# Attention convolutions from six products per four output columns, with the input planes stored by their producer

## The chip, the core and the metric

The kernel runs on one core of one Trainium2 chip, in one launch. The metric is the device time of that core in microseconds (us); lower is better. The core has a matrix engine (TensorE, called PE in the profile), a vector engine (VectorE, DVE), a scalar engine (ScalarE, ACT), a general engine (GpSimd, POOL) and a queue engine that here only issues transfers (SyncE, SP). Each works through its own list of instructions in order. TensorE reads its operands from the on-chip memory (SBUF) and writes into accumulator banks (PSUM); the other results go through SBUF. DRAM tensors are reached by DMA only.

## What is computed

Two layers are applied to four images of 96 channels by 128 x 128 pixels, all in float32. The first is a state-space block (projection, a 3x3 depthwise convolution, four scans over the image, a layer norm, an output projection). The second, where the change lies, is this, for every image on its own:

```python
def _attn_conv(x1, x2, aw1, aw2, aw3):          # C = 96, K = 3, pad = 1
    key = unfold_nonoverlap(conv2d(x1, aw1))    # 3x3 patches, 42 x 42 of them
    qry = unfold_nonoverlap(conv2d(x2, aw2))
    attn = einsum("bckl,bqkl->bqck", key, qry)  # one 96 x 96 matrix per tap
    attn = softmax(attn.reshape(B, C, C * 9) / sqrt(C * 9), axis=2)
    value = conv2d(x1, aw3)
    return conv2d(value, attn.reshape(B, C, C, 3, 3))   # weights of this image
xr, x1, x2 = relu_split_norm(x)
y1 = layer_norm(_attn_conv(x1, x2, aw1, aw2, aw3))
y2 = layer_norm(conv2d(x2, w_conv2)) * x1
out = xr + conv2d(concat([y1, y2]), w_full) + b_full    # 1x1
```

So an image needs five 3x3 convolutions of 96 to 96 channels: aw1 and aw3 on x1, aw2 and w_conv2 on x2, and the last one on `value`, with weights that are known only when the first four are done.

## The kernel before

**Two halves of the program.** In the first half the projections of the four images run beside the scans, then the output norm of image 0 (`ssm_output`, `split_norm`) and its four convolutions (`direct_maps`, nine plain taps) beside the rest of the scans. In this half `in_order` fixes each engine's list to the order of emission. In the second half each image b gets an `attention(b)` on the "left", and beside it a "light" stream: `attn_output(b-1)` (through `close`) and then `ssm_output(b+1)` and `split_norm(b+1)` (through `norm`). `co_run(left, right, pace)` interleaves the two: every generator yields the cost of what it has emitted, and the right one gets pace times the cost of the left one; whatever is left of the light stream is emitted alone afterwards. Here the framework's scheduler may move instructions, with the emission order as priority. Image 0 needs only the last convolution in its `attention`, as `direct_maps` has done the others (`img.mapped`).

**Convolutions before.** `attention` makes two output columns from four products in place of six taps' worth of multiplications. The 96 input channels times three rows (288 contraction rows) are stacked as 128 + 128 + 32 partitions. `load_rows` brings six rows of a padded map (`x1d`, `x2d`, `vd`: rows of PW = 129) into three tiles `y0`, `y1`, `y2`, already shifted by rows; `columns` makes the four column combinations in the tiles `t0`, `t1`, `t2`, on GpSimd (L1269 to L1271) and VectorE (L1276, L1278; for the value map L1269 too). `products` runs, for each of four products, two full matmuls (L1293, PSUM tile `bank`), and then the four 32-row rests in four row groups of the array (L1304). `outputs` copies one bank to SBUF on ScalarE (L1342) and combines four banks with four VectorE instructions (L1334 to L1337). A "pair set" of 12 rows of one map takes two passes with 128 output channels (one chunk of six rows each), and one with the other 64 channels of both chunks side by side in the array's columns. Weights carry `wd` in their name for the pairs and `wa` for the last convolution. The float32 matmul shows as two instructions in the trace.

**Attention matrix.** `Taps` keeps the key and query rows in `ring` tiles, turns nine rows of patches at a time (`turned`: 18 transposes per group, L1388, copied by ScalarE as `kt`, L1393) and multiplies them (`multiplied`, L1403, added to `sm` by L1414). `weights` takes the softmax and makes the product weights; the last pass of the w_conv2 channels is held back (`taps.rest`) and emitted between the softmax and the transposes of the weights.

**PSUM.** In the second half the left pool has six tiles of one bank (`bank`), and the light stream's pool two.

**split_norm.** It has two loops over 16 pieces of eight rows: one for the sums (L1082 to L1089), one that writes the positive half `x1` and the negative half `x2` (ScalarE L1165, VectorE L1170, store on ScalarE's DMA queue).

Of the kernel before, what the change touches and what calls it, by code (L numbers as in the profile page):

```python
# [17 lines left out]
C = 96  # L18
H = W = 128
L = H * W  # L20
CH = 512
# [8 lines left out]
PW = W + 1  # L30
AR = 12
CR = AR // 2
GROUP = 9
NG = H // GROUP
RING = 4 * GROUP // 3
NSTRIP = (H + AR - 1) // AR

# [25 lines left out]
def kernel(  # L63
# [853 lines left out]
    def ssm_output(b, yms, xnew, stats, ps, side):  # L917
# [5 lines left out]
        with tc.tile_pool(name="c2", bufs=2, side=side) as p2:  # L923
# [10 lines left out]
            def squares(c):  # L934
                sq = p2.tile([C, 2, SN], F32, name="sq", bufs=1)
                for j in range(2):
                    nc.scalar.activation(sq[:, j], ys[c][:, j], AF.Square)
                sums_of[c] = sq, bank(ps)

            def sums(c, j):  # L940
                sq, pm = sums_of[c]
                for g in range(4):
                    nc.tensor.matmul(
                        pm[32 * g : 32 * g + 32],
                        lhsT=mean192[:, 0:32],
                        rhs=(ys[c], sq)[g % 2][:, j, bass.ts(g // 2, CH)],
                        start=(j == 0),
                        stop=(j == 1),
                    )

# [50 lines left out]
            for c in range(NS + 2):  # L1001
# [5 lines left out]
                if new:  # L1007
                    squares(c)
# [30 lines left out]
    def split_norm(xnew, x1d, x2d, stats, keep, cnt, ps, side):  # L1039


        with tc.tile_pool(name="n2", bufs=2, side=side) as p2:
            ahead = []

            def piece(t):
                if t < NS:
                    y = p2.tile([C, SN], F32, name="xn", bufs=4)
# [29 lines left out]
            later = Later()  # L1077
            for i in range(NS):
# [9 lines left out]
                z = p2.tile([C, SN], F32, name="xz")  # L1088
# [3 lines left out]
            later.flush()  # L1092
            for i in range(3):
# [62 lines left out]

            for i in range(NS):
# [3 lines left out]
                for side_, m in ((0, x1d), (1, x2d)):  # L1161
                    h = p2.tile([C, RS, PW], F32, name=f"half{side_}")
                    nc.gpsimd.memset(h[:, :, 0:1], 0.0)
                    to = h[:, :, 1:PW]
# [8 lines left out]
                    at = (i * RS + 1) * PW  # L1173
                    later(lambda m=m, at=at, h=h: nc.scalar.dma_start(
                        m[:, at : at + RS * PW], h.rearrange("p h w -> p (h w)")
                    ), 1)
                later.tick()
                yield 3.5
# [8 lines left out]


# [3 lines left out]
    def products_weights(wt, v, s):  # L1192

        nc.vector.tensor_copy(wt[:, :, 0:2], v[:, :, 0:3:2])
        nc.vector.tensor_add(s, v[:, :, 0], v[:, :, 2])
        nc.vector.tensor_scalar(s, s, 0.5, None, ALU.mult)
        for i, sign in ((2, 0.5), (3, -0.5)):
            nc.vector.scalar_tensor_tensor(wt[:, :, i], v[:, :, 1], sign, s, ALU.mult, ALU.add)

    def pair_weights():  # L1200
# [4 lines left out]
        with tc.tile_pool(name="wq", bufs=2, side="right") as pw:  # L1205
            for pair in ((aw1, aw3), (aw2, w_conv2)):
                g = pw.tile([C, 3, 3, 2, C], F32, name="g")
                for j, src in enumerate(pair):
                    v = src.rearrange("c (h w) o -> c h w o", w=3)
                    for w in range(3):  # L1210

                        nc.sync.dma_start(g[:, :, w, j], v[:, :, w if j else 2 - w])
                taps.append(g)
            yield
            for i, g in enumerate(taps):
                g = g.rearrange("p h w j o -> p h w (j o)")
                wt = pw.tile([C, 3, 4, 2 * C], F32, name="wt")
# [25 lines left out]
    def load_rows(pool, m, r0, r):  # L1243


        n = r * PW + 1
        tiles = [pool.tile([128, CR * PW + 4], F32, name=f"y{i}", tag=f"y{i}") for i in range(3)]
        for y, parts in zip(tiles, STACK[:2]):
            for p, c0, c1, dh, _ in parts:
                at = (r0 + dh) * PW  # L1250
                nc.sync.dma_start(y[p : p + c1 - c0, :n], m[c0:c1, at : at + n])
        at = (r0 + 2) * PW
        nc.sync.dma_start(tiles[2][0:32, :n], m[64:96, at : at + n])
        for p in range(32, 128, 32):
            nc.sync.dma_start(tiles[2][p : p + 32, : n - 1], m[64:96, at + 1 : at + n])
        return tiles

    def columns(pool, tiles, r, first):

        def of(t, k, p0=0, p1=128):  # L1260
# [717 lines left out]
```

## Time and profile before

| | |
|---|---|
| device time, three runs | 6721.16 us median (6720.42 to 6732.53) |
| profiled execution, first to last instruction | 6729.0 us; its time outside the span is not shown |
| PE busy | 5618.7 us (84%), 22236 matmuls |
| DVE busy | 4792.1 us (71%) |
| ACT busy | 2985.5 us (44%) |
| POOL busy | 3802.7 us (57%) |
| DMA | 1226.28 MB, mean 182 GB/s |
| mean granted PE clock | 0.900 |

Busy time is the time in which the engine executes at least one instruction; for PE the ends are modelled, so it is an upper view. The granted clock is the share of full speed that the matrix engine was allowed. The second half starts at about 3606 us; the image-specific convolution (weights `wa`) of images 0, 1, 2 and 3 runs at 3608 to 3812, 4654 to 4804, 5660 to 5820 and 6461 to 6609 us, and ahead of each of the last three lies the pairs stage of that image (from 3815, 4820 and 5840 us).

### The profile page before, as it was taken

To read this page: it belongs to the slowest core of one execution; us is meant where nothing else is said; L and a number is where in the kernel's file an instruction comes from. 1 tells how busy PE (TensorE), PEld (TensorE's weight loads), DVE (VectorE), ACT (ScalarE), POOL (GpSimd) and SP (SyncE) were. 2 spreads that over 40 slices of the span, in tenths; PEclk is the share of its full clock that TensorE was granted. 3 is DMA by queue.
4 is the path that set the end of the run, shared out by engine and by line. 5 is a ranking of instruction groups with operands and counts; after the bars stand their busy time and mean duration, and the time that the engine had idled before them with its cause. 6 is when DMAs were issued, how large, how long until landed. Compare 5 with 4: busy or idle time off the path is not lost. (4 is left out here: it accounts for less than half of the span.)

```text
span 6729.0 us, 74614 instructions
## 1 busy us (share of the span) xinstructions
PE 5618.7 (84%) x22236; PEld 2323.3 (35%) x22236; DVE 4792.1 (71%) x6588; ACT 2985.5 (44%) x3749; POOL 3802.7 (57%) x2568
## 2 busy tenths in 40 slices
PE   5989978878886618989996988987988987988987
PEld 2323323322221104444342433433333443334442
DVE  3257879979896578889537776658776658775578
ACT  1357767777875566677434112233122233121112
POOL 2236758879796438889423634545644445545561
PEclk9999989989996659999997989998989998999998
DMA  6766777866765666765668666657666657664566
GB/s 166 174 155 187 199 212 198 227 168 179 220 179 165 187 191 191 207 187 169 198 186 235 182 172 161 185 146 232 165 179 166 176 153 233 168 182 125 135 169 183
DMA packets 796126, 1226.28 MB, mean 182 GB/s; under 512 B 218702, under 2 KB 558678, under 8 KB 783244
## 3 DMA queue, kind: packets, MB, share of 16 engines
q1 hardware_dynamic: 761740, 1129.63, 61.7%
q10 hardware_dynamic: 17776, 53.47, 2.5%
q0 software_dynamic: 16208, 38.42, 2.1%
q8 instruction: 179, 2.93, 0.2%
q14 instruction: 223, 1.83, 0.1%
HBM read 856.79 MB, written 295.13 MB: 171 GB/s over the span
## 5 line engine op out<-in xcount | busy, mean ns | idle before, releaser
L615 PE MATMUL bank<-y,wp 128*128 128x512 f32 (+3 forms) x3584 | 1317.5, 625 | 72.4 <-DMA y<-y 34.2
L1293 PE MATMUL bank<-t,wd 128*128 128x384 f32 (+2 forms) x4224 | 1175.4, 507 | 61.6 <-ACT s L1342 23.0
L848 POOL TENSOR_TENSOR y<-y,dl 128x1024 f32<-128x1024 f32 x384 | 1054.5, 2746 | 244.9 <-DVE dl L840 220.4
L815 POOL TENSOR_TENSOR dl<-dl,u 128x1024 f32<-128x1024 f32 x384 | 1008.2, 2625 | 253.6 <-ACT dA L791 119.0
L1269 POOL TENSOR_TENSOR t<-y 128x768 f32<-128x768 f32 (+1 forms) x352 | 572.0, 1625 | 780.8 <-DMA y<-x1d 280.5
L836 DVE TENSOR_TENSOR_SCAN dA<-dA,pBC 128x512 f32<-128x512 f32 x768 | 981.7, 1278 | 31.5 <-DVE pBC L819 0.5
L1342 ACT COPY s<-bank 128x384 f32<-128x384 f32 (+2 forms) x292 | 135.5, 464 | 1718.8 <-PE bank L1304 1606.6
L1293 PEld LDWEIGHTS bank<-t,wd 128*128 128x128 f32 (+1 forms) x4224 | 579.9, 175 | 609.0 <-issue 352.5
L729 PE MATMUL pBC<-xr,wbc 60*128 60x512 bf16 (+1 forms) x1536 | 459.8, 402 | 354.3 <-DVE dA L836 281.0
L840 DVE TENSOR_TENSOR dl<-dA,pBC 128x512 f32<-128x512 f32 x768 | 528.8, 689 | 269.6 <-PE pBC L729 196.8
L615 PEld LDWEIGHTS bank<-y,wp 128*128 128x128 f32 (+3 forms) x3584 | 458.7, 169 | 742.2 <-issue 652.8
L1661 PE MATMUL bank<-y,wn 128*128 128x384 f32 (+5 forms) x2408 | 673.4, 507 | 40.5 <-ACT ring L1675 15.9
L1293 PE MATMUL bank<-t,wa 128*96 128x384 f32 (+1 forms) x1408 | 497.6, 500 | 97.0 <-POOL t L1270 36.0
L658 ACT ACTIVATE dl<-pd,dtb 128x512 f32<-128x512 f32 x768 | 485.6, 684 | 184.6 <-PE pd L729 169.4
L1270 POOL TENSOR_TENSOR t<-y 128x384 f32<-128x384 f32 (+1 forms) x440 | 457.1, 1039 | 147.3 <-DMA y<-vd 68.3
L819 DVE TENSOR_TENSOR pBC<-dl,pBC 128x512 f32<-128x512 f32 x768 | 527.1, 686 | 7.7 <-POOL dl L815 6.0
L1334 DVE TENSOR_TENSOR d<-s,bank 128x384 f32<-128x384 f32 (+2 forms) x292 | 156.1, 535 | 520.1 <-ACT s L1342 492.1
L1271 POOL TENSOR_TENSOR t<-y 128x384 f32<-128x384 f32 (+1 forms) x440 | 442.7, 1006 | 0.0
L1661 PEld LDWEIGHTS bank<-y,wn 128*128 128x128 f32 (+3 forms) x2408 | 308.1, 168 | 340.5 <-issue 172.4
L791 ACT ACTIVATE dA<-dl,negA 128x1024 f32<-128x1024 f32 x384 | 420.3, 1141 | 2.3
L729 PEld LDWEIGHTS <-wbc 60*128 60x128 bf16 (+1 forms) x1536 | 104.0, 96 | 789.3 <-issue 775.3
L658 ACT ACT_TABLE_LOAD x245 | 314.3, 1283 | 100.9 <-PE pd L729 93.9
(255 smaller groups left out, 7774.4 us busy)
## 6 DMA issues: line engine op xcount, KB each, us to landing
u<-zb SPq DMA_DIRECT2D x192, 1024.0 KB
yms<-y SPq DMA_DIRECT2D x96, 512.0 KB
y<-yms SPq DMA_DIRECT2D x64, 768.0 KB
xn<-xnew SPq DMA_DIRECT2D x128, 384.0 KB
y<-y SPq DMA_DIRECT2D x128, 258.2 KB
zb<-z SPq DMA_DIRECT2D x64, 512.0 KB
y<-vd SPq DMA_DIRECT2D x168, 193.8 KB
y<-in_x SPq DMA_DIRECT2D x56, 480.0 KB
```

The source lines that it names most:

```text
L615: nc.tensor.matmul(blocks(pz[p:e]), lhsT=ws[k][:, d, c : c + e - p], rhs=window(ys[k], at, d, n), start=(i == 0), stop=(i == len(terms) - 1),)
L658: nc.scalar.activation(dst, src, AF.Softplus, bias=bias)
L729: nc.tensor.matmul(p, lhsT=w[rows], rhs=xr[rows, at : at + CH], start=True, stop=True)
L815: nc.gpsimd.tensor_mul(t, t, u_view(n))
L819: nc.vector.tensor_mul(p, live[n]["dl"][:, bass.ts(half, CH)], p)
L836: nc.vector.tensor_tensor_scan(h, h, p, init, ALU.mult, ALU.add)
L840: nc.vector.tensor_mul(live[n]["dl"][:, sl], live[n]["dA"][:, sl], live[n]["C", half])
L848: nc.gpsimd.tensor_add(v, v, t.rearrange("p (a b) -> p a b", b=W))
L1269: eng.tensor_sub(v[:, 0:2], of(y, 0), of(y, 2))
L1270: nc.gpsimd.tensor_add(v[:, 2], of(y, 0)[:, 1], of(y, 2)[:, 0])
L1293: nc.tensor.matmul(pc[p:e, :n], lhsT=w[:, i, c : c + e - p], rhs=t[k][:, i, :n], start=(k == 0), stop=False,)
L1661: nc.tensor.matmul(pc[p:e, :n].rearrange("p (h w) -> p h w", w=W), lhsT=w[:, c : c + e - p], rhs=v[:, :, 0:W], start=(i == 0), stop=(i == ...
```

## The change

**Arithmetic.** Four output columns are made from six products (points 0, 1, -1, 2, -2 and infinity) where two were made from four. Every 3x3 weight becomes 3 x 6 (`NP = 6`) in place of 3 x 4.

**Producer makes the planes.** The six column combinations of an input map ("planes", 33 column groups each per row, with padding) are computed once by `planes_of`, four ScalarE scalings and seven GpSimd additions or subtractions per piece, and stored in DRAM tensors `x1p`, `x2p`, `vp` of [96, 6, 131, 33]. For images 1 to 3 `split_norm` does it for x1 and x2 (two maps, 16 pieces of eight rows), and `attention` does it for `value` (pieces of six rows). Image 0 keeps its maps as before; in its `attention` a new function `lift` reads `vd` in pieces of four rows and makes the planes.

**Consumer.** A chunk is 12 rows. Its loads are four: one of 96 channels x 6 planes x 14 rows into `ya`, one of 32 channels, and two small ones into `yc`; the second 128-row stack `yb` is made from `ya` by two ScalarE copies of 64 x 2376 elements. The load of chunk c + 2 is emitted after the last product of chunk c. `columns` and its instructions are gone.

**Products, PSUM and evacuation.** `products` runs four of the six, their rests, then two and their rests; PSUM on the left is three tiles of two banks. `outputs` takes one ScalarE copy of two banks, two VectorE instructions over two banks, then a few over one (see the diff). One temporary tile `sd`, one output tile `oc`.

**Attention matrix.** Patches are turned six rows at a time (21 groups where there were 14), the two maps' transposes share one PSUM tile and one ScalarE copy; the products of two groups accumulate in PSUM. Nothing is held back for the softmax any more.

**Around it.** `squares` makes one half at a time in a single half-size tile (its second half after the first sums); `xn` has three buffers for four and `xz` one for two; channel order in the 32 + 64 split is swapped; 18 stores of zeros are added near the start; the pace of the light stream is 0.85 where it was 0.6.

```diff
+TW = 4; NP = TW + 2; TN = W // TW; PT = TN + 1; PP = PT * TW; AA = 2.0
...
-            def squares(c):
-                sq = p2.tile([C, 2, SN], F32, name="sq", bufs=1)
-                for j in range(2):
-                    nc.scalar.activation(sq[:, j], ys[c][:, j], AF.Square)
+            def squares(c, j):
+                sq = p2.tile([C, SN], F32, name="sq", bufs=1)
+                nc.scalar.activation(sq, ys[c][:, j], AF.Square)
...
             def sums(c, j):
...
+                if j == 0:
+                    squares(c, 1)
...
+            def stored(i, m, h):                       # split_norm
+                if planes:
+                    return planes_of(
+                        later, p2, h, RS, lambda pl: store_planes(nc.scalar, m, i * RS, RS, pl)
+                    )
...
-                later.tick()
-                yield 3.5
+                for _ in range(6 if planes else 1):
+                    later.tick()
+                    yield 2.0 if planes else 3.5
...
+    def planes_of(later, pool, t, r, then, most=RS):
...
+            nc.scalar.mul(eo, by_k(1), a2)
+            nc.gpsimd.tensor_sub(df, by_k(2, TW), by_k(0, TW))
...
+            nc.scalar.mul(pl[:, 0:NP:5], df[:, 0:2], a2)
+            nc.scalar.mul(pl[:, 3], df[:, 1], AA)
+            nc.gpsimd.tensor_sub(eo, by_k(3), eo)
+            nc.gpsimd.tensor_add(pl[:, 1], eo[:, 1], eo[:, 0])
+            nc.gpsimd.tensor_sub(pl[:, 2], eo[:, 1], eo[:, 0])
...
+            nc.gpsimd.tensor_sub(pl[:, 0:NP:5], df[:, 2:4], pl[:, 0:NP:5])
+            nc.gpsimd.tensor_sub(pl[:, 4], df[:, 2], pl[:, 3])
+            nc.gpsimd.tensor_add(pl[:, 3], df[:, 2], pl[:, 3])
+            then(pl)
...
+        a, b = pairs_of(ps), pairs_of(ps)              # products
+        to = {1: a[:, 0], 3: a[:, 1], 2: b[:, 0], 4: b[:, 1]}
+        for i, _ in FOUR:
+            main(to[i], i)
+            later.tick()
+            yield 1.3 * share
+        rest(0, FOUR, to)
+        sums, finish = evac
+        sums(a, b)
...
+        c = pairs_of(ps)
+        to = {0: c[:, 0], 5: c[:, 1]}
+        for i, _ in TWO:
+            main(to[i], i)
...
+        rest(1, TWO, to)
+        finish(c)
...
+                nc.scalar.copy(got[0][:, 0], a[:m, :, :n])      # outputs
...
+                nc.vector.tensor_sub(d, s, b[:m, :, :n])
+                nc.vector.tensor_add(s, s, b[:m, :, :n])
+                for p, e, v in parts:
+                    for k, x, f in ((1, d, AA), (2, s, AA * AA)):
+                        nc.vector.scalar_tensor_tensor(
+                            at(v, k), rows(x[p:e, 1]), f, rows(x[p:e, 0]), ALU.mult, ALU.add
+                        )
+                nc.vector.tensor_add(s[:, 0], s[:, 0], s[:, 1])
+                nc.vector.scalar_tensor_tensor(
+                    d[:, 0], d[:, 1], AA * AA * AA, d[:, 0], ALU.mult, ALU.add
+                )
...
+                    nc.vector.tensor_add(
+                        to,
+                        got[0][p:e, :, 0].rearrange(of, t=TN),
+                        c[p:e, :, :n].rearrange(of, t=TN),
+                    )
...
+                    for p, e, c0, h, k in ((0, 96, 0, 0, 2), (96, 128, 64, 1, 1)):   # load
+                        to = ya[p:e, :, : (r + k) * PT]
+                        src = maps[m][c0 : c0 + e - p, :, r0 + h : r0 + h + r + k]
+                        nc.sync.dma_start(to, src.rearrange("c i h t -> c i (h t)"))
...
+                    yb = p2.tile([128, NP, AR * PT], F32, name="yb")                 # turn
+                    for h in (1, 2):
+                        nc.scalar.copy(
+                            yb[64 * h - 64 : 64 * h, :, :n], ya[0:64, :, h * PT : h * PT + n]
+                        )
...
+            def lift(i):
...
+                for a in range(r0, r0 + r, 4):
+                    h = p2.tile([C, 4 * PP + 4], F32, name="lift")
...
+                    own(planes_of(
+                        own, p2, h, 4, lambda pl, a=a: store_planes(nc.sync, img.vp, a, 4, pl), 4
+                    ))
...
-    psl = ctx.enter_context(tc.tile_pool(name="psa", bufs=6, space=PSUM, side="left"))
+    psl = ctx.enter_context(tc.tile_pool(name="psa", bufs=3, space=PSUM, side="left"))
...
-        co_run(left, light, 0.6 if b else 1.5)
+        co_run(left, light, 0.85 if b else 1.5)
```

## Prediction

> **What bounds the kernel now.** I read the page first, then the windows of image 1's two stages, then the groups and waits inside them, then the timeline. Windows (stretch, length, busy time and count of PE, PEld, DVE, ACT, POOL; granted clock; DMA share; GB/s) of its pairs stage and its last convolution:
>
> ```profile
> 3820.00:4640.00 820.00, 695.60 (x3124) 324.56 (x3122) 538.70 (x783) 236.70 (x333) 350.57 (x351) 0.91 0.64 173
> 4654.00:4804.00 150.00, 145.81 (x526) 62.72 (x528) 134.65 (x196) 15.89 (x27) 111.52 (x97) 0.99 0.71 200
> ```
>
> TensorE is busy 85% and 97% of the two, ScalarE 29% and 11%. The groups of the whole page that the change cuts (busy us, mean ns; idle before them and its releasers):
>
> ```profile
> L1293 PE MATMUL bank<-t,wd 128*128 128x384 f32 (+2 forms) x4224 | 1175.4, 507 | 61.6 <-ACT s L1342 23.0 <-DVE s L1335 19.1 <-DVE sm L1414 16.2
> ...
> L1293 PE MATMUL bank<-t,wa 128*96 128x384 f32 (+1 forms) x1408 | 497.6, 500 | 97.0 <-POOL t L1270 36.0 <-DMA wa<-ring 24.4 <-DVE t L1276 11.9
> ```
>
> Waits of the pairs stage (who for whom: us, times, longest):
>
> ```profile
> POOL t L1269 <- DMA y<-x1d: 111.2, 7, 26.6
> ...
> PE bank L1403 <- ACT kt L1393: 24.1, 13, 7.7
> ...
> PE bank L1765 <- DVE c L1754: 21.0, 10, 4.0
> ```
>
> and those of the SP queue:
>
> ```profile
> SPq L1486 <- DVE ring L1337: 170.7, 16, 18.2
> ```
>
> TensorE waits in many small pieces, on PSUM copies and on VectorE. GpSimd waits for loads, 26.6 us at the longest, behind an SP queue that stores hold for up to 18.2 us; TensorE hardly feels it, since columns are made ahead. Last, the timeline of the last convolution:
>
> ```profile
> 4779.97 2.82 PE L1293 MATMUL bank<-t,wa 128*96 128x384 f32 x8
> 4782.72 0.89 PE L1304 MATMUL bank<-t,wa 32*96 32x384 f32 x4
> 4783.53 2.82 PE L1293 MATMUL bank<-t,wa 128*96 128x384 f32 x8
> ```
>
> From start to start, eight instructions take 2.75 us and two rests 0.81, without a gap: 12 rows take 4 x 3.56 = 14.2 us.
>
> **What the Trainium skill says.** "TensorE: Matmul & The Clock Gate", Part 3 (packing small matmuls): matmuls in different row or column groups of the array run together. The trace agrees: 32 instructions of 64 columns took 5.38 us where 16 of 128 took 5.33. "SBUF — State Buffer", "SBUF: two separate sides": a VectorE instruction with two SBUF inputs and a GpSimd one lock each other out for their whole length. It agrees: L1276 takes 0.48 to 0.57 us where I looked at single ones, and 1.05 in the mean of the pairs stage. "GPSIMD Engine Reference", 3.1: about 2.6 cycles an element with two inputs, 2.2 ns at the page's 1.2 GHz. Here it is less: in the pairs stage L1270 (384 elements) takes 0.974 us and L1269 (768) 1.566, so 1.54 ns an element and 0.38 us per instruction, which I use.
>
> **TensorE.** Six products per four columns stream 0.75 of the columns of four per two: 0.25 x (1175.4 + 497.6) = -418 us, that is 98 in each of three pairs stages and 31 in each of four last convolutions. The rests (L1304) go from one group per two columns to two per four: nothing. Patches of six rows make 378 transposes and 189 multiplications an image for 252 and 126; L1388 and L1403 are busy 43.0 and 33.2 us in image 1's stage, so half more is 38. The marginal time is less (five transposes 0.82 us, four 0.62), some 26. I take 35: 63 remain per pairs stage, -189 in all.
>
> **VectorE.** Gone: L1276 and L1278, 94 us in the pairs stage and 40 in the last convolution, with 23 of L1269 there. Added, per 12 rows of 128 outputs: three instructions of 768 elements, estimated 0.95 us each (0.537 for 384 and 0.679 for 512 in L1334 and L994), and four of 384 out of SBUF at 0.6 to 1.0; 5.3 to 6.9 against 4.3. The pass of 64 takes 2.8 to 5 against 2.1. Per set of 12 rows of one map 10.7 us of old work becomes 8 to 12. So VectorE gets no relief beside `attn_output`, whose L1753 to L1760 (101 us) and L1766 (23) fill it: TensorE's gain is partly lost there, +10 a stage (0 to 20): +30.
>
> **GpSimd.** Gone: 302 us of columns in the pairs stage (L1269 to L1271), 114 in the last convolution. Added: eight rows of planes are 3168 elements in seven instructions, 7.5 us, x 32 = 241 an image; value planes 22 x 6.3 = 139. The sum falls, but it moves: the second `split_norm` loop emits 192 units for 56, so the light stream (463, against 526 x 0.85 = 447) now lasts through the last convolution, and 16 units remain to run alone: about 10 us twice, +20 (0 to 40). Image 0: `lift` is 32 x 5.1 = 163 us of GpSimd, and some 60 of image 1's planes come late, against a stage of 204 us: -30 to +40, I take 0.
>
> **ScalarE.** Added per image: `yb`, 66 copies of 2376 elements; 0.464 us for 384 and 1.048 for 1024 give 0.91 ns an element, 2.3 us each, 152 us. Plane scalings 77, `kt` 10, the value's 32-channel copy 16: 255 on 253. TensorE keeps its old cover only while the PSUM copy comes in time, and now `yb` waits for a load on the engine that also empties PSUM, with the light stream's instructions behind it and TensorE waiting for a tile. Between a rest and the next need of its tile lie 2 to 6 us of matmuls. Price: 0 to 145 us an image (all of GpSimd's waits on x1d and x2d loads, 111.2 and 33.5). I take 20, as loads are asked for some 25 us ahead in the pairs: +60. The three PSUM tiles of two banks belong to this term.
>
> **Loads and the last convolution.** Loads carry 1.5 MB per 12 rows in four issues, where 2.4 MB went in 16; SP gets lighter. But with two `ya` the load of chunk c + 2 waits for the end of chunk c. Landing takes about 3 us (192 KB 3.7, 384 KB 4.3) and 1.5 MB takes 5.0 to 8.6 us (at 299 GB/s, the busiest slice of the pairs stage, to 173); then come 4.6 of `yb`. TensorE needs 3 x 2.75 + 2 x 0.81 = 9.9 us a chunk. Two chunks per (12.6 to 16.2) + 9.9: 11.3 to 13 each, 124 to 143 us for 148. That is -15 for image 3. For 1 and 2 the light stream's planes (some 17 pieces, 128 us of GpSimd) and the single `oc` tile make it 13 to 15 a chunk: 0 (-20 to +15 each).
>
> **Rest.** The pass kept back for the softmax (7.3 us) no longer covers it: 3 x 8 = +24. Halved `squares` put a wait of ScalarE on TensorE into image 0's norm, where the order is fixed: 0 to 3 us x 16 pieces, I take 1: +16. Zero stores are 10368 packets of 132 bytes on SP; at the mean 87 ns (61.7% of 16 x 6729 us over 761740) 0 to 56 us, I take 15. Fewer `xn` and `xz` buffers, swapped channels, product weights: 0, hidden by the slow steps of `split_norm`; without that cover 10.
>
> **Sum.** -189 + 30 + 20 + 60 - 15 + 24 + 16 + 15 = -39. The profiled span, 6729.0, is 7.8 us (0.1%) over the median of the runs; no time outside it is shown. Put on the median: 6721 - 39, about 6680 us.
>
> **Rivals.** All of TensorE's gain arrives: -189 - 124 + 55 (softmax, squares, zeros), 6460 us. For it: no other engine's sum exceeds TensorE's. Against: the load chain above. Slower, by ScalarE's order: the PSUM copy into `sd` stands behind the next chunk's `yb`, which stands behind its load, and half of GpSimd's 145 us reaches TensorE, 72 x 3 = 216 in place of 60: 6680 + 156, about 6840. It decides from 0.9 us of stall a chunk on (99 us over 110 chunks). For it: the wait of 26.6 us; against it: the lead of 25. GpSimd bounds the second `split_norm` loop: 15 us for a piece of both maps against about 14 of other work, 48 pieces, +48: 6730. That the change doesn't do what it says I exclude: the counts are in the code.
>
> **Numbers.** A measurement of this kernel can tell about 0.2% (13 us) from no change. Chances: the likeliest 0.35 (own range 6560 to 6705), the full gain 0.14, GpSimd's or another even balance 0.07, ScalarE's order or several prices at their upper ends 0.44. The range, 6470 to 6890, reaches from nearly the full gain over the slower case.
>
> **What would show it.** Right: the main matmuls of pairs and last convolutions busy near 1255 us together; transposes 1386 for 1008; ScalarE over half busy in the pairs stages; last convolutions at 11 to 15 us a chunk. Wrong: TensorE waiting for the copy into `sd` for more than 60 us a stage (slower), last convolutions at 9.9 us a chunk (faster), or image 0's stages longer by more than 40.

## Result and the profile after

The change makes the kernel slower: 6996.59 us (6989.58 to 7007.83, four runs) against 6725.15 (6720.42 to 6732.53, four runs), a ratio of 1.0402 with a 95% interval of 1.0386 to 1.0417. The forecast was 6680, and the range ended at 6890. The profiled spans are 6987.6 and 6729.0 us.

Where the 258.6 us between the two spans lie follows from the first and last main matmul of each stage in the two traces (us). The stage times ahead of the prediction were coarser: by this count image 0's last convolution before ends at 3802 us, image 2's lies at 5654 to 5805, and image 3's pairs begin at 5821. The last two columns belong to experiments and are used further down.

| stage | before | after | two GpSimd operations | all planes on VectorE |
|---|---|---|---|---|
| start of image 0's last convolution | 3608 | 3637 | 3642 | 3626 |
| image 0, last convolution | 193 | **367** | 265 | 251 |
| image 1, pairs stage | 823 | 817 | 727 | 802 |
| image 1, last convolution | 150 | **181** | 140 | 157 |
| image 2, pairs stage | 817 | 785 | 695 | 740 |
| image 2, last convolution | 151 | **180** | 141 | 157 |
| image 3, pairs stage | 628 | 612 | 550 | 572 |
| image 3, last convolution | 145 | 128 | 129 | 130 |
| six gaps between the stages | 93 | 155 | 186 | 180 |
| after the last of them | 121 | 127 | 132 | 128 |

Image 3's last convolution, with no planes beside it, got 17 us shorter, as forecast. The pairs stages gained 6, 32 and 16 us, where TensorE's term promised 63 each. The last convolutions of images 1 and 2 grew by 31 and 29 us. Image 0's, priced at nothing, alone lost 174 us, and it begins 29 us later: its first matmul waits 20.5 us for the load of planes that `lift` has just stored.

The page's first line of after, and the windows of image 1's pairs stage, its last convolution, and image 0's last convolution (columns as in the prediction: stretch, length, busy time and count of PE, PEld, DVE, ACT, POOL, granted clock, DMA share, GB/s):

```profile
PE 5408.1 (77%) x23256; PEld 2373.8 (34%) x23256; DVE 4667.8 (67%) x6155; ACT 3838.1 (55%) x4426; POOL 3828.8 (55%) x2988
```

```profile
4028.00:4846.00 818.00, 655.80 (x3610) 348.17 (x3610) 518.03 (x747) 406.08 (x457) 354.60 (x388) 0.85 0.59 154
4880.00:5060.00 180.00, 130.00 (x392) 55.75 (x391) 136.17 (x121) 99.05 (x96) 158.37 (x157) 0.82 0.68 175
3637.00:4005.00 368.00, 137.23 (x396) 57.68 (x396) 138.56 (x125) 159.18 (x206) 335.68 (x490) 0.64 0.58 150
```

In the two last convolutions GpSimd is busy 88% and 91% of the time, TensorE 72% and 37%. In the kernel before TensorE had 97% of image 1's. VectorE was about as long busy (136 us for 134.65), with 121 instructions, many of them larger, where it had 196.

Image 0's last convolution waits for loads of the planes that `lift` stores (who for whom: us, times, longest):

```profile
PE two L1380 <- DMA ya<-vp: 172.4, 8, 42.6
```

The main matmuls' groups of after (busy us, mean ns; idle before them and who ended it):

```profile
L1380 PE MATMUL two<-ya,wd 128*64 128x192 f32 (+3 forms) x2376 | 606.9, 437 | 136.2 <-DVE ring L1466 54.0 <-DVE sm L1554 21.4 <-ACT kt L1650 18.4
L1380 PE MATMUL two<-yb,wd 128*64 128x192 f32 (+3 forms) x2376 | 576.2, 418 | 9.9 <-ACT yb L1786 9.9
...
L1380 PE MATMUL two<-ya,wa 128*96 128x384 f32 (+1 forms) x528 | 263.6, 587 | 357.5 <-DMA ya<-vp 172.4 <-DVE oc L1466 56.8 <-ACT sd L1456 56.0
...
L1380 PE MATMUL two<-yb,wa 128*96 128x384 f32 (+1 forms) x528 | 247.7, 556 | 34.2 <-ACT yb L1786 34.2
```

These rows can't be added up, as `ya` and `yb` matmuls overlap at every change from one to the other. Taken together, the main matmuls are busy as follows, before (L1293) and after (L1380; columns: stretch, length, busy time and count of PE, the same of PEld, granted clock, DMA share, GB/s):

```profile
3600.00:6740.00 3140.00, 1672.98 (x5632) 800.48 (x5632) 0.91 0.64 175
3637.00:6862.00 3225.00, 1398.47 (x5808) 762.21 (x5808) 0.82 0.58 150
```

So 1398 us, where 1255 were forecast and 1673 were used before. The timeline of image 3's last convolution shows why it isn't less:

```profile
6781.17 1.59 PE L1380 MATMUL two<-ya,wa 128*96 128x384 f32 x2 [3.03 <-ACT sd L1456]
6782.55 1.49 PE L1380 MATMUL two<-yb,wa 128*96 128x384 f32 x2
6783.83 0.96 PE L1380 MATMUL two<-ya,wa 128*96 128x384 f32 x2
...
6785.28 0.81 PE L1380 MATMUL two<-ya,wa 128*96 128x384 f32 x2
6785.92 0.81 PE L1380 MATMUL two<-yb,wa 128*96 128x384 f32 x2
```

After a stall of 3.03 us the first four matmuls start 0.64 to 0.69 us apart (means of two), later ones 0.32. The Trainium skill, "TensorE: Matmul & The Clock Gate", Part 1, says that an idle array falls to half rate and needs some microseconds of work to leave it; this trace agrees: its clock record shows half rate for 3.41 us, from 6780.72 on, which is inside the stall. So a stall costs more than its own length, and the granted clock of the pairs stage fell from 0.91 to 0.85 although TensorE did less. In the whole trace 1346 of the 5808 main matmuls start at half rate, before it was 413 of 5632.

The waits of image 1's last convolution (who for whom: us, times, longest), where before it was ScalarE that waited for TensorE:

```profile
DVE sd L1441 <- ACT sd L1456: 32.3, 8, 9.4
...
PEld two L1380 <- ACT sd L1456: 28.6, 9, 8.8
ACT eo L1328 <- POOL pl L1338: 26.3, 7, 4.3
```

and the SP queue of the pairs stage, which used to wait for VectorE's ring and now waits for GpSimd's planes:

```profile
SPq L1352 <- POOL pl L1345: 162.9, 22, 12.8
```

### The profile page after: what moved, and what is told of

Read it like the earlier page. It is cut to its first block, busy times and chain, and to the rows that moved or that the text cites. A ratio compares the mean times of both kernels' runs of the same rounds, so it can differ in the third digit from the quotient of the medians.

```text
span 6987.6 us, 74482 instructions
## 1 busy us (share of the span) xinstructions
PE 5408.1 (77%) x23256; PEld 2373.8 (34%) x23256; DVE 4667.8 (67%) x6155; ACT 3838.1 (55%) x4426; POOL 3828.8 (55%) x2988
## 4 chain that ended last, share of the span: by engine, by line
PE 27%; POOL 18%; issue 17%; DVE 16%; DMA 11%; ACT 9%; SPq 2%; ACTq 0%; DVEq 0%; POOLq 0%
PE bank L620 11%; PE bank L1956 5%; DVE dA L841 5%; POOL df L1329 4%; PE two L1380 3%; POOL pl L1343 3%; DVE pBC L824 2%; POOL eo L1336 2%; PE pBC L734 2%; DVE dl L845 2%; ACT yb L1786 2%; POOL pl L1345 2%; POOL pl L1338 2%; POOL pl L1337 2%; POOL pl L1344 2%
## 5 line engine op out<-in xcount | busy, mean ns | idle before, releaser
L1380 PE MATMUL two<-ya,wd 128*64 128x192 f32 (+3 forms) x2376 | 606.9, 437 | 136.2 <-DVE ring L1466 54.0
L1786 ACT COPY yb<-ya 64x2376 f32<-64x2376 f32 (+1 forms) x220 | 467.9, 2127 | 267.3 <-DMA ya<-x2p 105.8
L1380 PE MATMUL two<-yb,wd 128*64 128x192 f32 (+3 forms) x2376 | 576.2, 418 | 9.9 <-ACT yb L1786 9.9
L1380 PE MATMUL two<-ya,wa 128*96 128x384 f32 (+1 forms) x528 | 263.6, 587 | 357.5 <-DMA ya<-vp 172.4
L1441 DVE TENSOR_TENSOR sd<-sd,two 128x384 f32<-128x384 f32 (+5 forms) x176 | 137.4, 780 | 554.6 <-ACT sd L1456 541.9
L1336 POOL TENSOR_TENSOR eo<-vt,eo 96x396 f32<-96x396 f32 (+1 forms) x66 | 89.2, 1352 | 656.6 <-ACT eo L1328 656.6
L1380 PEld LDWEIGHTS two<-ya,wd 128*64 128x64 f32 (+1 forms) x2376 | 276.5, 177 | 396.5 <-issue 181.4
L1195 DVE SCALAR_TENSOR_TENSOR half<-xn,thr,half 96x1024 f32<-96x1024 f32 x128 | 212.9, 1675 | 259.0 <-ACT half L1190 134.5
```

Source lines behind the costliest of these rows:

```text
L1380: nc.tensor.matmul(of(to[p:e], r), lhsT=w[:, i, c : c + e - p], rhs=tiles(t[k][:, i], o, r), start=(k == 0), stop=False,)
L1786: nc.scalar.copy(yb[64 * h - 64 : 64 * h, :, :n], ya[0:64, :, h * PT : h * PT + n])
```

## The experiments

The theories in order of their appearance: **A**, ScalarE's list (its scalings wait for GpSimd, and PSUM copies stand behind them); **B**, GpSimd's time for a piece; **C**, GpSimd and VectorE hold each other up at the SBUF reads. Each median below stands beside about 6720 us for the kernel before and 6997 for the changed one.

### Which part of the change costs

Of the seven GpSimd and three ScalarE operations of `planes_of` (the code has three scalings, not four), two GpSimd subtractions stay, so the planes hold other numbers and only the time means anything:

```diff
-            nc.scalar.mul(eo, by_k(1), a2)
-            nc.gpsimd.tensor_sub(df, by_k(2, TW), by_k(0, TW))
...
+            nc.gpsimd.tensor_sub(pl[:, 0:TW], by_k(2, TW), by_k(0, TW))
+            nc.gpsimd.tensor_sub(pl[:, TW:NP], by_k(3), by_k(1))
```

> Edit: a piece of planes is made by two GpSimd subtractions (1584 elements for eight rows) in place of seven on GpSimd (3168) and four on ScalarE, so the planes hold other numbers; stores and loads are unchanged. This leaves out most of the arithmetic of the planes everywhere. GpSimd theory: image 0's stage falls below 220 us, the last convolutions of images 1 and 2 from 180 to 130 to 155, the kernel to 6680 to 6780. Rival (load chain and yb copies): image 0's stage stays above 300 us, the kernel above 6900. What is left above 6725 then is not the planes' arithmetic.

Measured: 6607.87 us, ratio to before 0.9836 (0.9818 to 0.9854). So the planes' arithmetic costs 389 us where it stands; the products, loads, `yb` copies and evacuation together would have been 1.6% faster than before. The table's column for this kernel shows that the 389 us lie in every stage with planes. Image 0's stage takes 265 us, not under 220: even this little work on GpSimd isn't free there.

The lift alone on VectorE (`planes_of(..., eng=nc.vector)` in `lift`, its seven operations):

> Edit: in image 0's lift the seven additions and subtractions per piece go to VectorE; everything else is the changed kernel (6996.6 us, image 0's last convolution 368 us with GpSimd busy 336 of it). GpSimd theory (that stage waits for planes that GpSimd makes one after another): about 150 us of GpSimd leave it, so it takes 230 to 270 us, and the kernel 6870 to 6910. Rival (the load of a chunk, its ScalarE copies and the order of ScalarE's list set the pace there): less than 30 us, 6965 to 6997.

Measured: 6940.03 us, 1.0329 (1.0305 to 1.0353). Image 0's last convolution takes 312 us, 55 less than in the changed kernel, which lies between the two forecasts. In that stage GpSimd's busy time fell from 336 to 235 us, but VectorE's rose from 138 to 271. More than the lift's GpSimd time is in the way.

Image 1's planes earlier, beside `direct_maps`:

```diff
-    co_run(left, next_norm, 1.0)
+    co_run(left, next_norm, 1.8)
```

> Edit: image 1's norm is emitted at 1.8 times the pace of the rest of image 0's plain convolutions, where it had 1.0, so that its planes are made before image 0's last convolution begins. GpSimd theory: the 27 of 32 pieces that GpSimd made inside image 0's last convolution move to a stretch where GpSimd was busy a quarter to a half; that convolution takes 170 to 220 us instead of 368, the stretch before it grows by 0 to 70, the kernel takes 6830 to 6920. Rival (load chain and ScalarE order): the stage stays above 320 us, the kernel within 30 us of 6997 or slower.

Measured: 7033.6 us, 1.0468 (1.0448 to 1.0488). Image 0's last convolution shrinks to 237 us, but starts 217 later. Both forecasts miss. `direct_maps` now ends at 3760 us instead of 3581, and in the 274 us before that convolution (3580 to 3854) GpSimd is busy 262 us, VectorE 68. There it is GpSimd's own length that counts.

`yb` by DMA instead of ScalarE's copies:

```diff
-                        nc.scalar.copy(
-                            yb[64 * h - 64 : 64 * h, :, :n], ya[0:64, :, h * PT : h * PT + n]
-                        )
+                        nc.sync.dma_start(
+                            yb[64 * h - 64 : 64 * h, :, : r * PT],
+                            src.rearrange("c i h t -> c i (h t)"),
+                        )
```

> Edit: the second stack yb is loaded from DRAM by two more transfers per chunk (2.1 MB a chunk and map instead of 1.5) and not copied by ScalarE. Rival of the prediction (ScalarE's order eats TensorE's gain): 152 us of ScalarE an image go, and with them the waits behind loads; each pairs stage loses 40 to 80 us, the last convolutions 20 each, the kernel takes 6700 to 6830. GpSimd theory: image 0's stage stays as it is and the pairs change by less than 15 us each; 6930 to 7000, or slower if the larger loads matter.

Measured: 7211.56 us, 1.0735 (1.0712 to 1.0758). Only image 3's pairs stage gains (563 us for 612); the others lose to the added transfers (last convolutions 208 for 180). So this run can't judge the prediction's slower rival, `yb` on ScalarE's list. The kernel with two GpSimd operations can: it keeps the `yb` copies and is faster than the kernel before.

### ScalarE's list

The three scalings moved to VectorE (`nc.vector.tensor_scalar(..., a2, None, ALU.mult)`):

> The three scalings of a piece's planes go from ScalarE to VectorE (tensor_scalar by a constant, the same numbers); GpSimd keeps its seven operations, the stores stay on ScalarE's queue. Theory A (ScalarE's list: its scalings wait for GpSimd's differences, and the PSUM copies sd<-two stand behind them, so that TensorE waits for ScalarE): first and second pairs stage 740 to 780 and 700 to 730 (817 and 785 in the changed kernel), the last convolutions of images 1 and 2 at 145 to 160 (180), total 6730 to 6850. Theory B (GpSimd's throughput is the bound): its work stays, the stages stay within 10 us, total 6950 to 7010.

Measured: 7193.12 us, 1.0697 (1.0669 to 1.0725): 196 slower than the changed kernel. Both theories miss: taking ScalarE out of the chain should have gained or done nothing. VectorE's scalings are stretched: the one for 528 elements that makes `eo` takes 1.28 us in the mean and 0.60 at the shortest, though it reads one operand only.

The same three moved to GpSimd:

> The three scalings of a piece's planes go from ScalarE to GpSimd itself, which then has ten operations for a piece and waits for nobody in between. By the rows of GpSimd's own operations of these sizes that is 1.7 + 1.4 + 0.9 = 4.0 us more for each of the 96 eight-row pieces and about 3.2 us for each of the 66 six-row pieces, some 600 us more on GpSimd in all, 110 to 140 of it in image 0's last convolution. Theory A (ScalarE's list): the pairs stages gain 30 us or more each all the same, because GpSimd has idle time there, and the last convolution of image 0 loses about 110: total 6900 to 7010. Theory B (GpSimd's throughput): every stage with planes gets longer, total 7150 to 7400.

Measured: 7643.16 us, 1.137 (1.1344 to 1.1396), 240 us above the upper end of B. Image 0's last convolution 546, image 1's stages 947 and 228. Image 3's pairs stage, with no x planes beside it, takes 618 for 612 (the 550 that a later expectation names for this run is the figure of the kernel with two GpSimd operations). A's gain of 30 us or more shows in no pairs stage. GpSimd is busy 694 us more than in the changed kernel, and the kernel takes 647 us more.

The x planes' stores moved from ScalarE's queue to GpSimd's (`store_planes(nc.gpsimd, ...)`), alone and with the scalings on VectorE:

> The stores of the x planes (store_planes in stored) are issued from GpSimd's queue instead of ScalarE's, nothing else. Theory A: one of ScalarE's three waits for GpSimd goes (the one for pl), 20 to 80 us less in all: 6915 to 6980. Theory B: GpSimd has 96 issues more, 6990 to 7040.

> Both edits together: scalings on VectorE, x-plane stores from GpSimd's queue, so that ScalarE waits for GpSimd nowhere in the planes. Theory A: 6680 to 6790, the pairs stages near those of the kernel with two GpSimd operations only (727, 695, 550). Theory B: 6950 to 7020. If VectorE becomes the bound instead, the first two pairs stages stay over 790.

Measured: 7040.98 us (1.0478, 1.0457 to 1.0499) and 7185.5 (1.0689, 1.0662 to 1.0716). In the second ScalarE waits for GpSimd nowhere in the x planes, and it is still 189 us slower. As its expectation said for the case that VectorE becomes the bound, the first two pairs stages stay over 790 (842 and 828). A as the main cause is refuted by the run with subtractions below: there ScalarE has no part in the planes' arithmetic, and the kernel is 277 us slower than the changed one.

### Work moved to VectorE

`df` stays on GpSimd; the other six go to VectorE with the scalings folded in:

```diff
-            nc.scalar.mul(pl[:, 0:NP:5], df[:, 0:2], a2)
-            nc.gpsimd.tensor_sub(pl[:, 0:NP:5], df[:, 2:4], pl[:, 0:NP:5])
+            nc.vector.scalar_tensor_tensor(
+                pl[:, 0:NP:5], df[:, 0:2], -a2, df[:, 2:4], ALU.mult, ALU.add
+            )
```

> GpSimd keeps one of a piece's seven operations (df, 2.25 us for an eight-row piece), VectorE gets the other six with the scalings folded in (scalar_tensor_tensor, (x times a constant) plus y), ScalarE has none of it. By VectorE's rows for these shapes in the kernel with the lift on VectorE (1.48 us for 528 elements, 0.83 for 264, 0.47 to 0.69 for 132) that is about 6 us an eight-row piece. Theory B1 (GpSimd's time for a piece sets the pace and no other engine is near): the last convolutions of images 1 and 2 go to 140 to 155 (180), image 0's to 250 or less, total 6640 to 6760. Theory B2 (VectorE is next in line: 136 us of other work in a last convolution and 17 pieces by 6 us make about 240): 205 to 240 for the last convolutions of images 1 and 2, total 7100 to 7350.

Measured: 6748.48 us, 1.0031 (1.0021 to 1.0042): 248 less than the changed kernel. B1 has the total right and comes near in the stages: image 1's last convolution takes 156 us (140 to 155 expected), image 0's 293 (250 or less). The operation for 528 elements takes 0.70 us there, not the 1.48 that B2 was reckoned with.

The pieces shared out between the two engines:

```diff
+                    vec = m is x1d and (planes == 1 or i % 3 == 1)   # these pieces on VectorE
...
+                                AR // 2, own=img.b == NB - 1,        # image 3: scalings on GpSimd
```

> The pieces are shared out by the room that each stage has: of image 1's planes (made beside image 0's last convolution) the x1 pieces go to VectorE with the scalings folded in, the x2 pieces stay on GpSimd and ScalarE; of images 2 and 3 every third x1 piece goes to VectorE; in image 3's pairs stage, with no next image beside it, the scalings of the value planes go from ScalarE to GpSimd. If the time of GpSimd for a piece sets the pace of image 0's last convolution (335 us of work in 367): 14 pieces by 9.1 us less, so 230 to 285. If it is the order of the lists or the lift's chain: over 310. Image 3's pairs stage: 545 to 570 (612 in the changed kernel, 550 where all scalings were on GpSimd). The others within 20 us. Total 6790 to 6870, or 6900 and more by the rival.

Measured: 6969.24 us, 1.0361 (1.0342 to 1.038). Image 0's last convolution takes 345 us, not 230 to 285, though by the trace VectorE makes 12 of the 23 eight-row pieces in it: sharing hardly helps (27 us in the whole kernel, beside 57 for the lift alone). Image 3's pairs stage takes 624, not 545 to 570.

Two of the six back on GpSimd, and all seven on VectorE (`nc.gpsimd.tensor_add` and `tensor_sub` for planes 1 and 2; `nc.vector.tensor_sub` for `df`):

> As the kernel with df on GpSimd and six operations on VectorE, but the two that make planes 1 and 2 out of eo (0.62 and 0.44 us on VectorE) are back on GpSimd, so that GpSimd has three operations of a piece, VectorE four, ScalarE none. In that kernel VectorE was busy 149 of 156 us in the last convolution of image 1 and 144 of 150 in the end of the pairs stage before it; 17 and 13 pieces by 1.06 us come off. Theory (the engine with the most work of a piece sets the pace; there VectorE): the last convolutions of images 1 and 2 at 138 to 147 (156), the pairs stages 10 to 20 shorter, image 0's last convolution 250 to 275 (293), total 6650 to 6700, under the kernel before. Rival (the hand-over between VectorE and GpSimd costs more than the work): 6740 to 6800.

> All seven operations of a piece on VectorE, none on GpSimd or ScalarE. Theory (VectorE is already the bound where pieces are made): 17 pieces by 2.2 us for df on top of 149 us give 180 to 195 in the last convolutions of images 1 and 2 (156 with df on GpSimd), image 0's 320 to 360 (293), total 6860 to 6960. Rival (the hand-over from GpSimd's df to VectorE is what waits): everything shorter than with df on GpSimd, total under 6740.

Measured: 6826.17 us (1.0158, 1.0139 to 1.0177) and 6765.96 (1.0066, 1.0049 to 1.0083). Relieving the fuller engine by 1.06 us a piece cost 78 us; loading it with everything cost about 17. VectorE's rows say why. The row that makes plane 3 or 4 of an eight-row piece (instruction form, count, busy us and mean ns), first with two operations back on GpSimd, then with none there:

```profile
L1345 DVE SCALAR_TENSOR_TENSOR pl<-df 96x264 f32<-96x264 f32 x192 | 129.7, 701 | 0.0
```

```profile
L1345 DVE SCALAR_TENSOR_TENSOR pl<-df 96x264 f32<-96x264 f32 x192 | 74.4, 421 | 0.0
```

The same instruction on the same data takes 0.70 us in the mean with GpSimd at work beside it and 0.42 without. That is neither work nor a wait for a result. It points to C.

### Held up where nobody waits

Two kernels test C directly. Both have all planes on VectorE. Beside each piece GpSimd works on a tile that no other engine touches: once five subtractions of two operands in SBUF, once thirteen fills that read nothing and take as long.

```diff
+        def beside():
+            scr = pool.tile([C, 2, most * PT], F32, name="scr", bufs=1)[:, :, :n]
+            still = zeros[0:C, 0:1].unsqueeze(2).to_broadcast([C, 2, n])
+            for _ in range(5):
+                nc.gpsimd.tensor_sub(scr, still, still)    # other kernel: 13 x nc.gpsimd.memset(scr, 0.0)
```

> All planes on VectorE (6766 us), and beside each piece GpSimd makes five subtractions of two broadcast zeros into a tile of its own (528, 396 or 264 elements, about 1.45 us for 528): some 7 us for a piece, about as much as the changed kernel gives GpSimd; nobody reads that tile and no engine waits for it, save GpSimd's own later work. Theory C (GpSimd and VectorE hold each other up when both read two operands in SBUF): VectorE's sd<-sd operations go from 0.46 back to 0.55 or more, its plane operations for 264 elements from 0.42 to 0.6 or more, the operation sd<-sd,two with one operand in PSUM stays at 0.78, total 6850 to 7000. Rival (only waits for GpSimd's results cost): durations and total as without it, 6740 to 6790.

> As the run with subtractions beside, but GpSimd fills its tile thirteen times (memset, about 0.53 us for 528 elements by the row of 1.17 us for 1292), the same 7 us for a piece, reading nothing. Theory C: VectorE's durations stay near those of the all-VectorE kernel, total 6740 to 6800, 60 us or more under the run with subtractions. If GpSimd's list is what costs (its own later work, xr and rd, comes late): as slow as the run with subtractions.

Measured: 7273.91 us (1.0825, 1.0806 to 1.0844) with the subtractions, 6761.67 (1.0063, 1.0043 to 1.0083) with the fills, 6765.96 without either. The durations are as C said, the total with the subtractions lies 270 us above its range. GpSimd's groups, subtractions and then fills:

```profile
L1328 POOL TENSOR_TENSOR scr<-zeros 96x528 f32<-96x528 f32 (+2 forms) x970 | 1215.4, 1261 | 69.3 <-DMA od<-oc 14.9
```

```profile
L1328 POOL MEMSET scr<- 96x264 f32 (+2 forms) x2522 | 1111.8, 458 | 108.6 <-DMA od<-oc 14.9
```

About the same busy time, 1215 and 1112 us; one costs 508 us and the other nothing. VectorE's timeline with the subtractions beside it:

```profile
4859.79 1.58 DVE L1348 SCALAR_TENSOR_TENSOR pl<-df 96x528 f32<-96x528 f32 x1
4861.30 1.29 DVE L1341 TENSOR_TENSOR pl<-eo 96x264 f32<-96x264 f32 x1
4862.51 1.29 DVE L1342 TENSOR_TENSOR pl<-eo 96x264 f32<-96x264 f32 x1
4863.72 2.50 DVE L1352 SCALAR_TENSOR_TENSOR pl<-df 96x264 f32<-96x264 f32 x2
```

and in the kernel without them:

```profile
4601.37 0.41 DVE L1335 TENSOR_TENSOR pl<-eo 96x264 f32<-96x264 f32 x1
4601.72 0.41 DVE L1336 TENSOR_TENSOR pl<-eo 96x264 f32<-96x264 f32 x1
4602.06 0.69 DVE L1341 SCALAR_TENSOR_TENSOR pl<-df 96x528 f32<-96x528 f32 x1
```

0.41 becomes 1.29 and 0.69 becomes 1.58: each gets 0.88 us longer, whatever its size. That is one hold-up for each instruction, not a lower speed. The two engines take turns: GpSimd's subtractions end at 4860.81, 4862.29 and 4863.50, VectorE's instructions at 4861.37, 4862.58 and 4863.79. And the hold-up follows the size of the GpSimd instruction: in this trace it is 0.87 us in the median beside subtractions of 528 elements, 0.65 beside 396 and 0.43 beside 264. Operations that read one operand from PSUM don't feel it: `sd<-sd,two` keeps its 0.78 us in the mean in all these kernels. The framework placed none of the subtractions in image 1's last convolution (GpSimd is busy 2.28 us there), and it takes 157 us, as without them; the last chunk but one of that image's pairs stage, with them, takes 77 us instead of 40.

The changed kernel has the same pattern without any added work. VectorE at 4710 us, then GpSimd:

```profile
4710.75 1.28 DVE L1195 SCALAR_TENSOR_TENSOR half<-xn,thr,half 96x1024 f32<-96x1024 f32 x1 [7.63 <-ACT half L1190]
```

```profile
4710.18 0.74 POOL L1337 TENSOR_TENSOR pl<-eo 96x264 f32<-96x264 f32 x1
4710.88 1.75 POOL L1338 TENSOR_TENSOR pl<-eo 96x264 f32<-96x264 f32 x1
```

Two equal GpSimd instructions: the first takes 0.74 us, the second 1.75, because VectorE's had started just before it and ran to 4712.03. So the delay goes both ways.

### What can be won back

With all planes on VectorE, the second products of the last chunk are put off into `taps.rest`, to run under the softmax as in the kernel before:

```diff
-                        yield from products(ps, jobs, pairs[m], later, evac)
+                        rest = products(ps, jobs, pairs[m], later, evac)
+                        if m and r0 + r == H:
+                            taps.rest = cover()     # rest, then load(c + 2)
```

> All planes on VectorE, and the second group of products of the pairs stage's last chunk (they go to oc and c2d, not into the rings that the softmax needs) is put off into taps.rest, so that TensorE makes it while the softmax runs, as in the kernel before. The three gaps of TensorE between the pairs stage and the last convolution, 42 us each with all planes on VectorE and 16 in the kernel before, shrink by 10 to 20 each: 6700 to 6740, about the kernel before. If VectorE, full with planes, sets the gap's end: 6750 to 6770.

Measured: 6745.29 us, 1.0039 (1.0026 to 1.0053). The gaps before the last convolutions of images 1 and 2 go from 42 to 21 and 22 us, but 21 us is all that the whole kernel gains: the three pairs stages take 13, 22 and 13 us longer.

On top of that, image 1's planes earlier, at a pace of 1.8 and of 1.3:

> All planes on VectorE and the softmax covered (6745 us), and the work on image 1's norm and planes beside direct_maps goes at a pace of 1.8 instead of 1.0, as in the run that lost 37 us with the planes on GpSimd. In the all-VectorE kernel VectorE was busy 76 of 180 us at the end of direct_maps and 281 of 283 in image 0's last convolution (252 us long). Theory C (GpSimd's reads were the trouble there): the last convolution goes to 150 to 190, of which 30 to 60 come back in direct_maps, total 6650 to 6715, under the kernel before. Rival (it is the order of ScalarE's and VectorE's lists beside direct_maps): the start of the last convolution is 100 us later or more, total over 6760.

> The same with a pace of 1.3. Theory C: about a third of the shift, the last convolution of image 0 at 210 to 235, total 6700 to 6735. Rival: over 6750.

Measured: 6777.57 us (1.0088, 1.007 to 1.0106) and 6733.27 (1.0012, 1.0001 to 1.0024). At 1.3 image 0's last convolution takes 246 us, not 210 to 235. At 1.8 it starts 151 us later and is 37 shorter, as the rival said, so theory C doesn't explain the loss of the earlier run with this pace, where GpSimd's own length was in the way. Here VectorE was busy 116 of the 120 us up to 3700, which suggests that its own work is simply too much there, but no run shows it. The best version stands 9 us above the kernel before and doesn't beat it.

## Why the prediction was wrong

**The step that failed** is the sum for VectorE and GpSimd: +30, +20, and 0 for image 0. The other terms add up to -89, which would have given 6632 us, and the kernel with two GpSimd operations, where the planes' arithmetic is nearly gone, took 6608. Two things were wrong in that step.

The first is an amount. Of image 1's planes "some 60" us were to come late, into image 0's stage. By the trace 23 to 24 of the 32 eight-row pieces fall in it, 207 us of GpSimd, beside 134 us for `lift`. That is more than the whole stage took before (194 us), so 0 couldn't hold.

The second is the lock. The prediction named it and then added up the two engines' times as if they could run side by side. The Trainium skill, "SBUF — State Buffer", "SBUF: two separate sides", says that a GpSimd instruction that reads SBUF and a VectorE one with two SBUF operands exclude each other for their whole length (the prediction left out that the GpSimd one must read). The runs with subtractions and with fills show it here, at 508 us against none. In the changed kernel the seven GpSimd instructions of each piece meet the new evacuation, which works out of `sd` in SBUF. The VectorE operations that appear equally often in the changed kernel and in the one with all planes on VectorE take 256 us longer in the former.

The traces allow an estimate of both together. Count every GpSimd instruction that reads SBUF, and every VectorE one with two SBUF operands, at the duration that the shortest tenth of its kind (operation, tiles, sizes) has in the same trace, and add the two engines up (us, rounded):

| stage (last convolution where nothing else is said) | GpSimd | VectorE | sum | length |
|---|---|---|---|---|
| before, image 0 | 100 | 70 | 170 | 194 |
| before, image 1 | 87 | 47 | 134 | 150 |
| after, image 0 | 299 | 58 | 357 | 367 |
| after, image 1 | 131 | 49 | 180 | 181 |
| after, image 2 | 131 | 49 | 179 | 180 |
| after, end of image 1's pairs (4680 to 4840) | 124 | 40 | 163 | 160 |
| lift on VectorE, image 0 | 189 | 137 | 326 | 313 |
| pieces shared out, image 0 | 207 | 123 | 331 | 346 |
| scalings on GpSimd, image 0 | 480 | 62 | 541 | 546 |

In the changed kernel the sum fills these stages within 3%. It also says why moving the lift to VectorE gave 55 us only: 110 us left GpSimd, and 79 came to VectorE. The estimate is good to some per cent, as one sum exceeds its stage.

The prediction's own trace had the lock in a stronger form. L1276's mean of 1.05 us in the pairs stage comes from a median of 0.54 and a few very long ones. In the longest, GpSimd's instructions follow each other without a gap, and VectorE's gets its turn only after the last of them:

```profile
4396.27 9.43 DVE L1276 TENSOR_TENSOR t<-y 64x384 f32<-64x384 f32 x1
```

```profile
4396.04 0.83 POOL L1271 TENSOR_TENSOR t<-y 128x384 f32<-128x384 f32 x1
...
4404.48 0.81 POOL L1271 TENSOR_TENSOR t<-y 128x384 f32<-128x384 f32 x1
```

**GpSimd, size and place.** An eight-row piece took 9.1 us, not 7.5; at the shortest durations it is 7.8, so the size was nearly right and the rest is hold-up. The total hardly changed, 1472 us of columns before and 1492 of planes. What counted was the crowding. The x planes and the lift's come in the second `split_norm` loop and in image 0's stage only, and in the last convolutions of images 1 and 0 GpSimd was busy 88 and 91% of the time. The prediction's own sign of being wrong, image 0's stages longer by more than 40, came true.

**TensorE, -189.** The main matmuls fell from 1673 to 1398 us, 143 short of the forecast 1255. Of that time 231 us before and 445 after ran at half rate. Counted at full rate (an estimate: half of these taken off), they are 1557 and 1176, a ratio of 0.755. So the quarter is there, and the shortfall is the clock after the stalls; the sum kept the old share of half rate. Where no next image's planes stood beside it, the term was nearly right: with all planes on VectorE image 3's pairs stage gained 56 us, against 63.

**ScalarE, +60, and the slower rival.** `yb` was right in size (2.13 us a copy, 2.3 forecast) and small in effect: image 3's pairs stage takes 49 us less without it, and 25 less with the scalings on VectorE. In the other stages moving work off ScalarE alone gained nothing worth the name.

**Right:** image 3's last convolution at 12 us a chunk (11.3 to 13); 1386 transposes; ScalarE at about half of the pairs stage (406 of 818 us). The softmax without cover was right in kind, but put at half its size: the gaps before the last convolutions of images 1, 2 and 3 grew by 18, 18 and 12 us, for 8 each. `squares` and zero stores, +16 and +15, cost nothing at the end: the last matmul of `direct_maps` ends at 3580.6 us before and at 3580.7 after.

**The last convolutions of images 1 and 2** were put at 0, at worst +15; they cost 31 and 29. With two GpSimd operations only they take 140 us: this, too, was the planes.

**What stays open.** Stage by stage the estimate doesn't tell the lock from GpSimd's own length: in image 0's stage GpSimd alone makes 299 of the 357 us. And no run moved the planes to a place where neither engine was full, so the 1.6% of the kernel with two GpSimd operations are not shown to be within reach.

## What to carry over

GpSimd's instructions that read SBUF and VectorE's with two SBUF operands are work for one resource: before adding up busy times, add these two up, stage by stage, and compare the sum with the stage's length. VectorE's one-operand scalings belong to the sum as well, going by the run that moved them there. Work moved between the two engines is little relief while both read SBUF; making all planes on VectorE in fewer instructions (`scalar_tensor_tensor` for a scaling and an addition) was worth 231 us here. To tell a lock from a wait, put work beside it that nobody waits for, once reading SBUF and once not.

## What was not expected of the hardware

- The hold-up of a VectorE instruction doesn't depend on its own size but on the GpSimd instruction beside it (0.43, 0.65 and 0.87 us for 264, 396 and 528 elements), and it strikes GpSimd as well (0.74 to 1.75 us).
- It isn't always one turn: in the kernel before, a VectorE instruction of 0.54 us in the median once waited out eight GpSimd instructions in a row, 9.43 us.
- Fills on GpSimd, 1112 us in all, cost VectorE and the kernel nothing.
- One eight-row piece takes 5.5 us on VectorE with the scalings folded in, and 9.1 on GpSimd plus 2.2 on ScalarE without.
- After a stall of 3 us matmuls ran at half rate until 3.4 us after the clock had been halved.
